# Attention scores in thirty-two-row products: sixteen 32 by 32 tiles of the TensorE array in place of four of 32 by 128

## The chip, the cores and the metric

The kernel runs on one core of a Trainium2 chip. The core has a matrix engine (TensorE, "PE" in the profile, with its weight loads shown as "PEld"), a vector engine (VectorE, DVE), a scalar engine (ScalarE, ACT), a general engine (GpSimd, POOL) and a sync engine (SyncE, SP) that here only issues DMA transfers. The metric is the device time of one execution in microseconds, as a median of several runs.

## What is computed

The reference is one block of a hybrid network on 16 sequences of 512 tokens by 256 features, all float32: causal attention with 16 heads of width 16, a routed feed-forward layer, a state-space scan, and the same routed layer once more, each on a layer-normalised input and added to the running `x`. The change touches attention alone:

```python
xn = x * rsqrt(mean(x * x) + EPS) * norm_w
q = (xn @ Wq.T + bq).reshape(B, T, H, hd).transpose(0, 2, 1, 3)
k = (xn @ Wk.T + bk).reshape(B, T, H, hd).transpose(0, 2, 1, 3)
v = (xn @ Wv.T + bv).reshape(B, T, H, hd).transpose(0, 2, 1, 3)
scores = einsum('bhqd,bhkd->bhqk', q, k) * scale
scores = where(causal, -inf, scores)
attn = softmax(scores, axis=-1)
out = einsum('bhqk,bhkd->bhqd', attn, v)
return xn + out.transpose(0, 2, 1, 3).reshape(B, T, D) @ Wo.T + bo
```

## The kernel before

**Order.** The program is written as a list of operations, each with an engine, a planned cost and the buffers that it reads and writes. `Plan.order` runs a small model of the engines over the list, and the operations are issued in the order that it picks, by due times written out in `STARTS` and `TURNS`. Each engine executes its own queue in that order. Attention of one sequence is thereby interleaved with the scan and the routed layers of the one or two before it. At the start, `Plan.resting` also adds some spare products (line 1056) that keep the array at work. Both use the planned costs, which are numbers in the source.

**Scores.** The 16 heads of a sequence are worked in four sets of four, and the sets in two pairs (the loop over `i`, line 723). For one set, queries and keys lie transposed in `qT` and `kT`: each of the four heads `g` has its own 32 partitions (`rows(g)`, line 517), so that a product over 32 partitions is one head's scores. Scores are computed twice. First with the queries' 128 rows as the stationary operand, for the row maxima (`maxima`, line 736, read by the VectorE reduction of line 749); then with the keys' 128 rows as the stationary operand and the maxima already subtracted in `qm`, for the exponentials (`weights`, line 685, read by the ScalarE exponential of line 689).

**The helper.** Both go through `filled` (line 635). It takes one buffer `sc` in PSUM, of 128 partitions by 4 heads by 512 columns, of which there is only one, and a list of one or two entries. An entry names a stationary block of 128 rows, a moving operand of `n` columns (512, 384, 256 or 128, because the causal triangle is skipped in blocks of 128), and a mask. For an entry, `score` (line 645) issues four products, one for each head; each writes all 128 partitions of that head's 512 columns. `masked` (line 652) then issues four bf16 products of 128 rows and 128 columns that add the causal mask on the diagonal block. Where the second entry has 128 columns, the mask is written first and the scores are added. The whole of a list is one operation of PE. It waits until the last reader of `sc` is done, and the reader (line 749 or 689) waits for the end of the operation.

For one pair of sets the lists are: four of one entry of 512 columns, four of 384 and 128 columns, and two of 256 and 256. That is 16 entries for one pair, 32 for a sequence and 512 in all, and each of the four widths occurs 128 times.

**Other products in small tiles.** The products of weights and values (line 672) and the sums of the scan (line 1020, and line 965 for its inputs) use 128 input partitions and 32 output rows: four tiles of the array side by side, each with its own 32 output partitions. Line 672 follows the exponentials; line 1020 follows GpSimd's product of line 1013.

Every float32 product above appears in the trace as two weight loads and two matmuls: line 647 has 2 x 2,048 of each for 512 entries of four products. Float32 transposes and the bf16 masks appear as one of each.

Of the kernel before, what the change touches and what calls it, by code (L numbers as in the profile page):

```python
# [17 lines left out]
P = 128  # L18
# [50 lines left out]
class Plan:  # L69
# [20 lines left out]
    def op(self, eng, cost, fn, r=(), w=(), lat=None, table=None, load=0.0, also=(), port=False, same=False):  # L90

        o = Op()
        self.slot += not same
        o.slot = self.slot
        o.eng, o.cost, o.fn, o.seq, o.num, o.table, o.load = eng, cost, fn, self.seq, len(self.ops), table, load
        o.lat = {"PE": 0.2, "SP": 2.0}.get(eng, 0.16) if lat is None else lat
        o.after, o.left, o.bufs = [], 0, []
        before = {}  # L100
        for things, writes in ((r, False), (w, True)):
            for thing in things:
                buf, part = thing if isinstance(thing, tuple) else (thing, None)
                if buf not in o.bufs:
                    o.bufs.append(buf)
                    buf.users += 1
                for p, (ws, rs) in buf.done.items():
                    if part is None or p is None or p == part:
                        for x in ws + (rs if writes else []):
                            before[x.num] = x  # L110
                ws, rs = buf.done.setdefault(part, ([], []))
                if not writes:
                    rs.append(o)
                elif part is None:
                    buf.done = {None: ([o], [])}
                else:
                    buf.done[part] = ([o], [])
        for buf in also:
            if buf not in o.bufs:
                o.bufs.append(buf)  # L120
                buf.users += 1
        before.pop(o.num, None)
        o.port, o.then, o.stage = port, None, self.stage
        for x in before.values():
            x.after.append(o)
            o.left += 1
        self.ops.append(o)
        return o
# [141 lines left out]
def tile_block(ctx: ExitStack, tc: tile.TileContext, a: dict, out: bass.AP):  # L270
# [4 lines left out]
    nc = tc.nc  # L275
# [6 lines left out]
    G = 4  # L282
# [218 lines left out]
    def psum(name):  # L501
        n, shape = banks[name]
        return plan.buf(name, lambda: ps.tile(shape, F32, tag=name, name=name, bufs=n))
# [13 lines left out]
    def rows(g):  # L517
        return slice(32 * g, 32 * g + 32)
# [10 lines left out]
    def pe(n, k=1, extra=0.02):  # L529

        return k * 2 * (n / 1200.0 + extra)
# [72 lines left out]
    def attention(b, x):  # L604
# [30 lines left out]
        def filled(todo, reads, into):  # L635


            sc = psum("sc")

            def run():  # L640
                for k, (lhsT, rhs, at, n, mask, diag) in enumerate(todo):

                    turned = k > 0 and n == P

                    def score():
                        for g in range(G):
                            nc.tensor.matmul(  # L647
                                sc()[:, g, at : at + n], lhsT=lhsT()[rows(g), :], rhs=rhs()[rows(g), :],
                                start=not turned, stop=turned,
                            )  # L650

                    def masked():
                        for g in range(G):
                            nc.tensor.matmul(  # L654
                                sc()[:, g, at + diag : at + diag + P], lhsT=identb, rhs=mask,
                                start=turned, stop=not turned,
                            )

                    for step in (masked, score) if turned else (score, masked):
                        step()  # L660

            return sc, op("PE", sum(pe(x[3], 1, 0.0) for x in todo) + (0.46 if len(todo) == 1 else 0.88 if todo[1][3] == P else 1.0), run, r=reads, w=[sc], also=into)
# [369 lines left out]
    for b in range(B):  # L1032
# [8 lines left out]
        n = NT // 2 if b == B - 1 else NT  # L1041
# [62 lines left out]
```

## Time and profile before

| what | value |
|---|---|
| time, median of 3 runs | 1951.58 us (1949.91 to 1952.15) |
| span of the profiled execution | 1952.9 us |
| mean granted TensorE clock | 0.968 |
| DVE busy | 1488.0 us (76%) |
| POOL busy | 1446.5 us (74%) |
| ACT busy | 1208.4 us (62%) |
| scores, line 647, matmul records | 4,096, of 210.3 + 211.8 us busy |
| masks, line 654, matmul records | 2,048, of 91.0 + 90.6 us busy |
| idle of PE just before line 647 | 54.2 + 45.3 us |
| DMA | 288.00 MB read, 26.21 MB written |
| instruction fetch of the largest queue (q8) | 105 packets, 1.72 MB |

The profile gives the span, from the first instruction to the last; of the profiled execution no separate time is shown. The span is 1.3 us above the median of the runs. "Busy" is the union of an engine's instructions, so that four products which run side by side count once. A row of a group gives the busy time of the whole group, the mean duration of one instruction in ns, and the idle time of its engine just before, with what ended it. Matmul durations include the time until the result has left the array.

### The profile page before, as it was taken

How to read it: one execution, taken by the hardware profiler on the slowest of the kernel's cores; microseconds unless marked ns; L12 is line 12 of the kernel's file. 1: busy time of each engine (PE TensorE's matmuls, PEld its weight loads, DVE VectorE, ACT ScalarE, POOL GpSimd, SP SyncE). 2: the span in 40 equal slices, each digit the busy share in tenths (PEclk: the TensorE clock that was granted, in tenths of full speed). 3: DMA queues.
4: the chain of work that ended last, by engine and by line, in shares of the span. 5: the costliest groups of instructions: out<-in, count | busy, mean ns of one | idle time of the engine just before them, and what ended most of it. 6: DMA issues, size and time to landing. Idle time of an engine off the chain costs nothing.

```text
span 1952.9 us, 34920 instructions
## 1 busy us (share of the span) xinstructions
PE 1710.2 (88%) x13337; PEld 953.1 (49%) x13337; DVE 1488.0 (76%) x2448; ACT 1208.4 (62%) x1618; POOL 1446.5 (74%) x846
## 2 busy tenths in 40 slices
PE   7889999999999989999899999999999999986445
PEld 5455445545454545545454555545454545544123
DVE  5245787879798887878798787879798787876553
ACT  2436466775757676675758576675758677573631
POOL 5102777878788887878788887878789787868893
PEclk9999899999999999999999999999999999998766
DMA  4002668768585768758585767768575877767891
GB/s 101 1 1 78 157 155 213 179 163 211 142 199 143 193 159 206 190 153 205 142 192 146 193 174 195 193 155 199 145 193 143 209 173 185 184 159 187 206 225 33
DMA packets 114568, 316.48 MB, mean 162 GB/s; under 512 B 17649, under 2 KB 38626, under 8 KB 114402
## 3 DMA queue, kind: packets, MB, share of 16 engines
q1 hardware_dynamic: 113554, 313.99, 65.1%
q8 instruction: 105, 1.72, 0.4%
q14 instruction: 61, 0.50, 0.1%
q10 hardware_dynamic: 848, 0.27, 0.1%
HBM read 288.00 MB, written 26.21 MB: 161 GB/s over the span
## 4 chain that ended last, share of the span: by engine, by line
PE 34%; DVE 25%; ACT 14%; issue 11%; POOL 10%; DMA 6%; SPq 0%; DVEq 0%; POOLq 0%; ACTq 0%
DVE dd L1010 10%; PE sc L647 7%; PE one L535 6%; PE one L579 6%; DVE negm L749 5%; DMA dd<-drows 5%; PE one L1020 5%; ACT one L1007 4%; PE one L672 4%; POOL dd L1013 4%; POOL dd L1002 3%; PE sc L654 2%; DVE st L542 2%; ACT xhR L555 2%; DVE x L594 2%
## 5 line engine op out<-in xcount | busy, mean ns | idle before, releaser
L1010 DVE TENSOR_TENSOR_SCAN dd<-one,dd 128x512 f32<-128x512 f32 x512 | 606.3, 1210 | 221.8 <-ACT one L1007 143.5
L1013 POOL TENSOR_TENSOR dd<-dd,bc 128x1024 f32<-128x1024 f32 x256 | 602.5, 2356 | 121.5 <-DVE dd L1010 55.4
L1002 POOL TENSOR_TENSOR dd<-dd,bc 128x1024 f32<-128x1024 f32 x256 | 604.1, 2361 | 86.3 <-DMA dd<-drows 63.0
L1007 ACT ACTIVATE one<-dd,am 128x512 f32<-128x512 f32 x512 | 345.7, 693 | 272.8 <-DVE dd L1010 136.0
L749 DVE TENSOR_REDUCE negm<-sc 128x4 f32<-128x1536 f32 (+3 forms) x224 | 368.1, 1667 | 68.4 <-PE sc L647 41.4
L647 PE MATMUL sc<-qm,kT 32*128 32x384 f32 (+3 forms) x2048 | 210.3, 480 | 54.2 <-ACT ptC L689 14.8
L647 PE MATMUL sc<-kT,qT 32*128 32x384 f32 (+3 forms) x2048 | 211.8, 482 | 45.3 <-DVE negm L749 43.6
L654 PEld LDWEIGHTS <-identb 128*128 128x128 bf16 x2048 | 115.4, 98 | 210.1 <-issue 210.1
L1020 PE MATMUL one<-dd,ysel 128*32 128x512 f32 x1024 | 153.1, 642 | 55.6 <-POOL dd L1013 49.3
L689 ACT ACTIVATE ptA<-sc 128x2048 f32<-128x2048 f32 x64 | 119.7, 1870 | 96.4 <-PE sc L654 96.4
L548 POOL TENSOR_SCALAR rs<-mv 128x4 f32<-128x4 f32 x64 | 12.4, 193 | 220.8 <-DVE mv L543 213.5
L647 PEld LDWEIGHTS sc<-qm,kT 32*128 32x128 f32 x2048 | 80.4, 183 | 134.7 <-ACT ptA L689 31.8
L647 PEld LDWEIGHTS sc<-kT,qT 32*128 32x128 f32 x2048 | 81.0, 183 | 128.2 <-DVE negm L749 56.4
L555 ACT ACTIVATE xhR<-x,nm,rs 128x256 f32<-128x256 f32 x192 | 102.3, 592 | 54.2 <-POOL nm L551 52.9
L689 ACT ACTIVATE ptB<-sc 128x2048 f32<-128x2048 f32 x64 | 120.0, 1875 | 23.7 <-PE sc L647 23.7
L535 PE MATMUL one<-base,xtR 128*128 128x256 f32 x496 | 133.9, 393 | 0.3 <-DVE dd L1010 0.2
L594 DVE TENSOR_TENSOR x<-one,x 128x512 f32<-128x512 f32 x126 | 83.8, 674 | 44.0 <-PE one L535 43.7
L542 DVE BATCH_NORM_STATS2 st<-x 128x6 f32<-128x256 f32 x256 | 103.2, 403 | 4.2 <-DMA x<-in_x_dram 2.5
L599 POOL TENSOR_TENSOR x<-x,bo 128x1024 f32<-128x1024 f32 x32 | 75.5, 2360 | 39.5 <-ACT xhA L555 30.5
L535 PEld LDWEIGHTS one<-base,xtR 128*128 128x128 f32 x496 | 92.2, 194 | 16.8 <-issue 1.7
L654 PE MATMUL sc<-mask_q,identb 128*128 128x128 bf16 x1024 | 91.0, 222 | 0.0
L654 PE MATMUL sc<-mask_k,identb 128*128 128x128 bf16 x1024 | 90.6, 221 | 0.0
(147 smaller groups left out, 2746.2 us busy)
## 6 DMA issues: line engine op xcount, KB each, us to landing
dd<-drows SPq DMA_DIRECT2D x512, 512.0 KB
x<-in_x_dram SPq DMA_DIRECT2D x16, 512.0 KB
drows<-dt SPq DMA_DIRECT2D x32, 256.0 KB
drows<-sg SPq DMA_DIRECT2D x32, 256.0 KB
bc<-brows SPq DMA_DIRECT2D x16, 512.0 KB
out_dram<-x SPq DMA_DIRECT2D x15, 512.0 KB
brows<-few SPq DMA_DIRECT2D x16, 64.0 KB
wo<-in_Wo_dram SPq DMA_DIRECT2D x2, 256.0 KB
```

Source lines behind the costliest of these rows:

```text
L535: nc.tensor.matmul(o[:, lo:hi], lhsT=lhsT, rhs=rhs, start=n == 0, stop=n == len(todo) - 1)
L542: nc.vector.bn_stats(st()[:, t, :], x()[:, t, :])
L555: op("ACT", act(256) + 0.23, lambda t=t: nc.scalar.activation(xh()[:, t, :], x()[:, t, :], AF.Identity, bias=nm()[:, t, 0:1], scale=rs()[: ...
L647: nc.tensor.matmul(sc()[:, g, at : at + n], lhsT=lhsT()[rows(g), :], rhs=rhs()[rows(g), :], start=not turned, stop=turned,)
L654: nc.tensor.matmul(sc()[:, g, at + diag : at + diag + P], lhsT=identb, rhs=mask, start=turned, stop=not turned,)
L689: o.then = op("ACT", act(G * 512), lambda: nc.scalar.activation(pt(), sc(), AF.Exp), r=[sc], w=[pt], table="exp")
L749: nc.vector.tensor_reduce(out, of, AX.X, ALU.max, negate=True)
L1002: op("POOL", pool(1024), lambda dd=dd: nc.gpsimd.tensor_tensor(dd()[:, :, 1, :], dd()[:, :, 1, :], both(0), ALU.mult), port=True, r=[(bc, ...
L1007: op("ACT", act(512) + 0.13, lambda i=i, k=k, dd=dd, dec=dec: nc.scalar.activation(dec(), dd()[:, i, 0, :], AF.Exp, scale=am[:, k + 4 * i ...
L1010: op("DVE", 1.13, lambda i=i, dd=dd, dec=dec: nc.vector.tensor_tensor_scan(dd()[:, i, 1, :], dec(), dd()[:, i, 1, :], 0.0, ALU.mult, ALU.a ...
L1013: op("POOL", pool(1024), lambda dd=dd: nc.gpsimd.tensor_tensor(dd()[:, :, 1, :], dd()[:, :, 1, :], both(1), ALU.mult), port=True, r=[(bc, ...
L1020: nc.tensor.matmul(sums()[rows(g), :], lhsT=ysel[:, m, :], rhs=four[g]()[:, g % 2, 1, :], start=m == 0, stop=m == 3)
```

## The change

In `score`, each head's product of 128 output rows becomes four products of 32 output rows. The stationary operand is cut to 32 columns, the output to 32 partitions; the moving operand is the same. The outer loop runs over the four blocks of output rows, the inner one over the four heads. The masks, the planned costs, the order of the operations and all waits between operations in the source are as before.

```diff
                     def score():
-                        for g in range(G):
-                            nc.tensor.matmul(
-                                sc()[:, g, at : at + n], lhsT=lhsT()[rows(g), :], rhs=rhs()[rows(g), :],
-                                start=not turned, stop=turned,
-                            )
+                        for h in range(0, P, 32):
+                            for g in range(G):
+                                nc.tensor.matmul(
+                                    sc()[h : h + 32, g, at : at + n], lhsT=lhsT()[rows(g), h : h + 32], rhs=rhs()[rows(g), :],
+                                    start=not turned, stop=turned,
+                                )
```

## The prediction

> **What bounds the kernel now.** I read the busy times first, then the chain of waits, then a table by stretches, then the score groups with their shapes kept apart.
>
> ```profile
> PE 1710.2 (88%) x13337; PEld 953.1 (49%) x13337; DVE 1488.0 (76%) x2448; ACT 1208.4 (62%) x1618; POOL 1446.5 (74%) x846
> ...
> PE 34%; DVE 25%; ACT 14%; issue 11%; POOL 10%; DMA 6%; SPq 0%; DVEq 0%; POOLq 0%; ACTq 0%
> ```
>
> PE is busiest, but the chain that ended last is shared among four engines. The 34% on PE are 664 us, or 0.39 of its 1710.2 us: if the chain stayed as it is, 0.39 of each microsecond added to PE would reach the end. A steady stretch, one sequence long (columns: length, then busy time and count of PE, PEld, DVE, ACT, POOL), says that the chain won't stay:
>
> ```profile
> 552.00:663.00 111.00, 102.32 (x832) 57.30 (x834) 92.62 (x152) 75.42 (x102) 91.36 (x53) 1.00 0.72 178
> ```
>
> PE is idle for only 8.7 of 111 us, so work added to it soon becomes the bound. The score products by width, and below them the tiles of 32 output rows that the kernel already has:
>
> ```profile
> L647 PE MATMUL sc<-kT,qT 32*128 32x512 f32 x512 | 74.0, 647 | 32.4 <-DVE negm L749 32.4
> L647 PE MATMUL sc<-kT,qT 32*128 32x384 f32 x512 | 59.4, 533 | 2.2 <-ACT ptB L689 1.6 <-DVE negm L749 0.4
> L647 PE MATMUL sc<-kT,qT 32*128 32x256 f32 x512 | 46.1, 426 | 10.7 <-DVE negm L749 10.7
> L647 PE MATMUL sc<-kT,qT 32*128 32x128 f32 x512 | 32.2, 321 | 0.0
> ...
> L672 PE MATMUL one<-ptA,vv 128*32 128x512 f32 x512 | 68.1, 603 | 9.0 <-DVE dd L1010 8.4
> L672 PE MATMUL one<-ptB,vv 128*32 128x384 f32 x512 | 54.2, 490 | 1.6 <-ACT ptB L689 1.6
> ```
>
> An entry (four products, two passes each) is 8 records, so 512 records are 64 entries: 74.0/64 = 1.156 us for 512 columns, 0.928 for 384, 0.720 for 256, 0.503 for 128. From 128 to 512 that is 0.653 us for 384 columns: 1.70 ns a column, 0.85 for each of two passes. The four heads therefore run side by side already. The tiles of 32 output rows do the same work in 68.1/64 = 1.064 and 54.2/64 = 0.847 us, some 0.08 less.
>
> **The change, part by part.** *Columns streamed.* Each of the sixteen tiles still streams n columns twice. If they overlap as the four do, the 1.70 ns a column stay: nothing is removed here, since the four heads filled all 128 rows of the array before.
>
> *Narrower weights.* A load brings 32 columns in place of 128. In the trace, the groups of eight loads look so:
>
> ```profile
> 603.35 0.31 PEld L647 LDWEIGHTS sc<-qm,kT 32*128 32x128 f32 x8 [0.17 <-issue]
> ...
> 601.33 0.16 PEld L1020 LDWEIGHTS one<-dd,ysel 128*32 128x32 f32 x8 [0.17 <-issue]
> ```
>
> The difference between the two rows of products, 0.08 us an entry, is what this saves. An isolated pair of groups agrees: 1.14 us for line 647 at 512 columns (599.48 us), 1.07 for line 1020 (601.33 us). I take -0.08.
>
> *Twelve more products, 24 more load and matmul pairs an entry.* In all 512 x 12 x 2 = 12,288 pairs, beside the 13,337 of now. The trace shows no entry with sixteen tiles, so this is bounded from both sides. The low end is the step from tile to tile in a burst that stands ready: eight loads of 110 ns take 0.16 us, so (160 - 110)/7 = 7 ns a step. Twelve more tiles start 12 x 7 = 84 ns later, and with -0.08 the entry stays as it is, about 0. The high end is the densest sustained row, the sixteen pairs of line 965: 398.02 to 398.49 us, where line 672 follows, or 29 ns a pair. That row is held by its 128 columns, so it is an upper bound of what the sequencer needs. At 29 ns with nothing queued ahead, the sixteenth product's first pass, pair 31 of 32, starts 30 x 29 = 870 ns late where the fourth tile's now starts 20 ns late: +0.85 - 0.08 = +0.77 us an entry.
>
> Between these stand the records of the sequencer's own waits. In more than a dozen sequences, four transposes of line 782 lie between two of them and pass in 74 ns: 18.5 ns a pair. In eight of twelve places where line 647 is followed by line 1020, sixteen pairs pass in 285 to 315 ns, about the same. At such waits at most 16 to 17 loads stood ahead of the array. I take these, because they measure the supply itself: of an entry's 32 pairs 17 stand ready while PE waits for `sc`, and the last first pass is (31 - 17) x 18.5 = 259 ns late. Per entry +0.259 - 0.020 - 0.08 = **+0.16 us**; for 512 entries +81 us of PE time.
>
> *What lies beside it.* An entry doesn't end before its last tile, and the masks can't start before. PE stands in its own order, so everything queued behind the entry waits too: masks, then whatever transpose, projection or scan sum the plan put there. The reader of `sc`, line 749 or 689, comes 0.16 us later for one entry and 0.32 for two; then the next score operation, which needs `sc` free. No DMA is moved and no queue of SP or POOL passed. Instruction fetch grows by 24,576 instructions; 1.72 MB for 26,674 is 64 bytes each, so 1.6 MB more, 0.4% of DMA time now and 0.8% after. I cost it at nothing, its cover being the seventeen loads that stand ready.
>
> *How much reaches the end.* Between 0.39 (the chain as it is) and 1 (PE bounds everything). I take 0.65: PE's 8.7 us of idle in 111 would take in some of the 81/16 = 5.1 us a sequence, but half of that idle, 56.3 us in all, is line 647 waiting for line 749, which the change puts off too. 81 x 0.65 = +53 us. The profile's span of 1952.9 lies 1.3 us above the median; 1951.6 + 53 = **2005 us**. Its own range, with 0.08 to 0.20 us an entry and 0.39 to 1: 1967 to 2054.
>
> *Two rules against the trace.* The trace first: at 257.87 us the third product of line 1020 waited for GpSimd, and the loads came in two fours, so both passes of the first two products stand in the queue before the third:
>
> ```profile
> 257.87 0.14 PEld L1020 LDWEIGHTS one<-dd,ysel 128*32 128x32 f32 x4 [0.33 <-issue]
> 258.85 0.14 PEld L1020 LDWEIGHTS one<-dd,ysel 128*32 128x32 f32 x4 [0.84 <-POOL dd L1013]
> ```
>
> Yet in line 647 four first passes start before any second one: within 603.30 to 603.50 us the trace has four matmuls in 0.60 us, each of 0.585. So a product passes over another tile's waiting second pass. The Trainium skill, "TensorE: Matmul & The Clock Gate", Part 3, says that matmuls start and end strictly in program order. By the trace the sum stands as above; by the rule each block of 32 rows would hold up the next, which is the second rival's price. The same page, Part 1, puts the least distance from start to start at about 25 ns; the 7 ns step above contradicts it for different tiles. By it, with nothing ready, an entry would gain 30 x 25 = 750 less 100 ns, 0.65 us, and the kernel 333 us of PE time. Its Part 3 also reports 10.6 times the speed for sixteen tiles of one pass at 4 ns a tile, which no run here shows.
>
> **The rivals.** *One: not slower.* If the supply keeps up with the burst, the step of 6 to 7 ns decides. 12 x 6 = 72 ns against 0.08 to 0.09 saved is -0.02 us an entry, -10 us of PE, -6 at the end: 1946; at 7 ns, no change. For it: one of the twelve places shows sixteen pairs in 131 ns, 8 ns a pair. It decides from about 8 ns a pair down: (31 - 17) x 8 = 112 ns less the 100 leave +0.012 us an entry, 6 us of PE, 4 at the end.
>
> *Two: the tiles of one head wait for each other.* If a second pass holds up the next block of rows in the same 32 partitions, the blocks form a chain of five passes in place of two. The columns of all entries are 128 x (512 + 384 + 256 + 128) = 163,840; three passes more at 0.85 ns are +418 us of PE, at 0.9 to 1 near the end: 2330 to 2370. For it: no trace of this kernel has more than three second passes waiting while a first one overtakes. Against it: tiles that share all input rows (line 1020) and tiles that share all output rows (line 647) both overlap. That the compiler lays the sixteen in fewer tiles would look the same, with other shapes in the rows.
>
> *Three: nothing stands ready.* If the queue is empty at each entry, because instructions are fetched too slowly or the doubled count eats the lead, the last first pass is 30 x 18.5 = 555 ns late: +0.455 us an entry, +233 us of PE, at 0.65 to 0.8: 2103 to 2138. Against it: PE waits for `sc` before many score operations, and the queue fills meanwhile.
>
> **How the numbers follow.** The forecast has 0.52; rival one 0.20, of which half is faster by over 0.2% and 0.08 within it; rival two 0.12; rival three 0.16. Some 0.2% (3.9 us) is what a measurement of this kernel can tell from no change. Faster 0.10, same 0.08, slower 0.82. The range reaches down to rival one's 1946 and up to just past rival three, 2145; it leaves out rival two and what lies below, under 0.2.
>
> **What would show it.** Right: line 647 with shapes 32*32 and 8,192 matmul records for each of its two pairs of operands; sixteen first passes of an entry of 512 columns begun within 0.2 to 0.3 us, and an entry 0.1 to 0.2 us longer than 1.156; PE's busy time up by some 80 us; idle before lines 749 and 689 for PE longer. Wrong towards rival one: sixteen starts within 0.11 us. Towards rival two: starts in fours, one pass apart, 2.1 us for 512 columns. Towards rival three: even steps of 18 ns or more for pairs through a whole entry, with "issue" before line 647. The share of 0.65 is wrong if PE's busy time rises as said and the span by much more or less.

## The result and the profile after

The changed kernel takes 1986.48 us (1985.95 to 1989.6), beside 1951.19 us before: 35 us more, a ratio of 1.0186 with a 95% interval of [1.0173, 1.0199]. The forecast was 2005 with a range of 1946 to 2145. Direction and range held; the reason did not. (The two profiled spans differ by less, 31.3 us: in the other runs a span lies about 2 us below its execution's time, so the profiled execution of the kernel before, with a span of 1952.9 us, was some 3.5 us longer than the median.)

The page of the changed kernel: span, busy time of the engines, the queue that brings PE's instructions (packets, MB, share of DMA time) and the chain of waits.

```profile
span 1984.2 us, 59496 instructions
...
PE 1727.9 (87%) x25625; PEld 919.9 (46%) x25625; DVE 1489.6 (75%) x2448; ACT 1210.7 (61%) x1618; POOL 1450.3 (73%) x846
...
q8 instruction: 201, 3.29, 0.8%
...
PE 37%; DVE 22%; ACT 16%; issue 13%; POOL 10%; DMA 3%; SPq 0%; DVEq 0%; POOLq 0%; ACTq 0%
```

The 96 additional packets of q8, of 16,384 bytes or 256 x 64 each, are just the 24,576 additional instructions.

PE's busy time rose by 17.7 us, not by 81, and its idle time by 13.6: together the 31.3 us by which the span grew. The scores by width, now at line 648 (64 entries a row), below one row of before:

```profile
L647 PE MATMUL sc<-qm,kT 32*128 32x128 f32 x512 | 32.2, 321 | 0.0
...
L648 PE MATMUL sc<-kT,qT 32*32 32x512 f32 x2048 | 74.3, 599 | 31.5 <-DVE negm L750 31.5
...
L648 PE MATMUL sc<-kT,qT 32*32 32x384 f32 x2048 | 60.2, 493 | 2.4 <-ACT ptB L690 1.9 <-DVE negm L750 0.5
...
L648 PE MATMUL sc<-kT,qT 32*32 32x256 f32 x2048 | 46.2, 386 | 10.9 <-DVE negm L750 10.9
...
L648 PE MATMUL sc<-qm,kT 32*32 32x128 f32 x2048 | 35.5, 282 | 16.5 <-issue 16.5
...
L648 PE MATMUL sc<-kT,qT 32*32 32x128 f32 x2048 | 32.1, 280 | 0.0
```

The rows of `kT,qT` stood at 74.0, 59.4, 46.1 and 32.2 us before. An entry of sixteen tiles takes as long as one of four. The row of `qm,kT` at 128 columns does not: 35.5 where it was 32.2 us, and 16.5 us of idle time before it that no instruction's end explains ("issue"), where there was none.

One undisturbed entry, first a stretch of 0.12 us at its start and then its weight loads:

```profile
611.15 0.60 PE L648 MATMUL sc<-qm,kT 32*32 32x384 f32 x16
...
611.15 0.23 PEld L648 LDWEIGHTS sc<-qm,kT 32*32 32x32 f32 x32 [0.17 <-issue]
```

All sixteen first passes, of 505 ns each, lie within 0.60 us: (600 - 505)/15 = 6 to 7 ns from start to start. The 32 loads take 0.23 us. And one disturbed entry (start, length, group):

```profile
432.64 0.62 PE L655 MATMUL sc<-mask_k,identb 128*128 128x128 bf16 x8
433.19 0.49 PE L648 MATMUL sc<-qm,kT 32*32 32x128 f32 x29
436.11 0.41 PE L648 MATMUL sc<-qm,kT 32*32 32x128 f32 x3 [2.43 <-issue]
436.45 0.66 PE L709 MATMUL one<-ident,avs 128*128 128x128 f32 x4
```

PE stops after 29 of 32 matmuls of one entry and goes on 2.4 us after the last of them has ended, 2.7 us after its start. The stretches around it (length, then busy time and count of PE, PEld, DVE, ACT, POOL; last the clock, the DMA share and GB/s):

```profile
425.00:433.30 8.30, 6.58 (x159) 3.76 (x143) 6.95 (x18) 8.29 (x11) 6.05 (x4) 1.00 1.04 243
433.30:434.60 1.30, 0.38 (x29) 0.12 (x28) 0.88 (x1) 0.09 (x1) 1.30 (x2) 1.00 0.73 173
434.60:436.10 1.50, 0.00 (x0) 0.00 (x0) 0.00 (x0) 0.00 (x0) 1.50 (x1) 1.00 0.07 22
```

For 8 us the scan's transfers hold all 16 DMA engines (share 1.04). At 433.30 us a packet of PE's instructions starts, the first since 424.9 us. Then PE, VectorE and ScalarE all stand still; GpSimd works on. The other long stops look alike: at 197.0, 659.0, 885.0 and 1101.7 us a packet starts, from 1.0 us before the last matmul ahead of the stop to 0.2 us behind it, and PE goes on 2.7 to 2.8 us after that start, though a packet itself takes 1.26 us.

How much of the 31.3 us is this? I took for every score entry the time from its first to its last matmul start, and what it has over the shortest entry of its width. Worked out from single records:

```
columns   before: shortest, sum over it    after: shortest, sum over it
128         232 ns    0.2 us                 233 ns   19.6 us
256         339 ns    0.6 us                 340 ns    0.6 us
384         445 ns    0.2 us                 446 ns    5.7 us
512         552 ns    0.7 us                 553 ns    5.5 us
```

The undisturbed entries are equal to 1 ns. The disturbed ones have lost 31.4 us, beside 1.7 before: 29.7 us of the 31.3 by which the span grew. 28.6 of the 31.4 lie in the entries for the exponentials. Not all of it is idle time, since matmuls that began before a stop run on; 17.3 us are (total, times, longest):

```profile
PE sc L648 <- issue: 17.3, 10, 2.7
```

Single records also tell where PE stops. Number all records of PE (weight loads, matmuls and its own waits) in the order of their starts. The eight gaps of over 1 us inside entries come after record 5,569, 12,225, 18,625, 25,025, 31,169, 37,569, 43,969 and 50,369. Each of these is 193 more than a multiple of 256, the number of instructions in a packet. So the stops lie whole packets apart, at the places where one packet ends and the next begins.

### The profile page after: what moved, and what is told of

Its sections match the earlier page's. It is cut to its first block, busy times and chain, and to the rows that moved or that the text cites. A ratio compares the mean times of both kernels' runs of the same rounds, so it can differ in the third digit from the quotient of the medians.

```text
span 1984.2 us, 59496 instructions
## 1 busy us (share of the span) xinstructions
PE 1727.9 (87%) x25625; PEld 919.9 (46%) x25625; DVE 1489.6 (75%) x2448; ACT 1210.7 (61%) x1618; POOL 1450.3 (73%) x846
## 4 chain that ended last, share of the span: by engine, by line
PE 37%; DVE 22%; ACT 16%; issue 13%; POOL 10%; DMA 3%; SPq 0%; DVEq 0%; POOLq 0%; ACTq 0%
PE sc L648 9%; DVE dd L1011 8%; PE one L535 6%; PE one L579 6%; DVE negm L750 5%; PE one L1021 5%; POOL dd L1014 4%; ACT one L1008 4%; PE one L673 4%; PE sc L655 3%; POOL dd L1003 3%; DMA dd<-drows 3%; DVE st L542 2%; ACT ptB L690 2%; DVE x L594 2%
## 5 line engine op out<-in xcount | busy, mean ns | idle before, releaser
L648 PE MATMUL sc<-qm,kT 32*32 32x512 f32 (+3 forms) x8192 | 222.6, 444 | 72.5 <-issue 17.3
L648 PE MATMUL sc<-kT,qT 32*32 32x256 f32 (+3 forms) x8192 | 212.8, 439 | 44.8 <-DVE negm L750 42.9
L648 PEld LDWEIGHTS sc<-qm,kT 32*32 32x32 f32 x8192 | 64.3, 103 | 153.7 <-issue 36.8
L648 PEld LDWEIGHTS sc<-kT,qT 32*32 32x32 f32 x8192 | 61.9, 103 | 128.1 <-DVE negm L750 53.3
```

Of the source, the lines that this page charges most:

```text
L648: nc.tensor.matmul(sc()[h : h + 32, g, at : at + n], lhsT=lhsT()[rows(g), h : h + 32], rhs=rhs()[rows(g), :], start=not turned, stop=turned,)
```

## The experiments

Theory A: PE's instructions come too late. The change nearly doubles their bytes, packets are held up while the scan's transfers fill the DMA engines, and PE runs dry in the dense score products. The rivals: every pair has a price of its own (B), entries pay by their width, the narrow ones most (C), blocks of one head hold each other up (D), sixteen narrow tiles cost time as such (E), instruction fetch is too slow even without other traffic (F), the number of instructions alone sets the loss (G).

**A third of the pairs.** The step of the loop over rows, and the size of the slices, is 64:

```diff
-                        for h in range(0, P, 32):
+                        for h in range(0, P, 64):
```

> Score products of 64 output rows: eight in place of four, 4,096 load and matmul pairs more than before (a third of what the change adds). Theory A (instruction packets that come late behind the data transfers stop PE for 2 to 3 us at a time): packets rise from 105 to about 137, so PE runs dry seldom; stalls inside score groups sum to 0 to 5 us and the time is 1945 to 1957 us. Theory B (every additional pair has its price in the entry where it stands): a third of +35, so 1960 to 1966 us.

Measured: 1945.29 us beside 1950.74, ratio 0.9974 [0.9965, 0.9984]: faster than the changed kernel, and by 0.3% than the one before. 137 packets, stalls inside score groups 1.6 us. Its maxima entries:

```profile
L648 PE MATMUL sc<-kT,qT 32*64 32x512 f32 x1024 | 72.3, 619 | 32.4 <-DVE negm L750 32.4
...
L648 PE MATMUL sc<-kT,qT 32*64 32x384 f32 x1024 | 57.7, 507 | 2.2 <-ACT ptB L690 1.8 <-DVE negm L750 0.5
L648 PE MATMUL sc<-kT,qT 32*64 32x256 f32 x1024 | 44.9, 407 | 10.8 <-DVE negm L750 10.8
...
L648 PE MATMUL sc<-kT,qT 32*64 32x128 f32 x1024 | 30.4, 293 | 0.0
```

72.3/64 = 1.130 us where it was 1.156, and so for each width: 0.02 to 0.03 us an entry. A narrower load is gained and only four more tiles are to be started. PE's busy time falls by 13.4 us (1710.2 to 1696.8), the time by 5.5: 0.41 reaches the end. B, which wanted +9 to +15, falls.

**One width alone.** The narrow tiles where `n == 512`, and where `n == 128`, in two kernels:

```diff
+                        size = 32 if n == 512 else P
-                        for h in range(0, P, 32):
+                        for h in range(0, P, size):
```

> Thirty-two-row products in the 128 entries of 512 columns alone: 3,072 pairs more than before. Theory A: packets about 129, hardly a stall, time within 4 us of before (1947 to 1956). Theory B: a quarter of +35, 1957 to 1963. Theory C (entries pay by width, because second passes of narrow ones come before the supply): under 2 us, since 512 columns give the supply the longest time.

> Thirty-two-row products in the 128 entries of 128 columns alone: 3,072 pairs more than before, as many as with 512 columns alone. Theory A: as with 512 alone, within 5 us of before, because the number of instructions is the same. Theory B: +9 us. Theory C: the 19.6 us that the groups of 128 columns lose in the changed kernel stay, 1965 to 1975.

Measured: 1949.86 (ratio 0.9994 [0.9982, 1.0007]) and 1951.99 us (1.0007 [0.9995, 1.0019]), neither to be told from before. In the second, all 128 entries of 128 columns take 233 or 234 ns from first to last start, where the changed kernel loses 19.6 us: C falls.

**The loops exchanged.**

```diff
-                        for h in range(0, P, 32):
-                            for g in range(G):
+                        for g in range(G):
+                            for h in range(0, P, 32):
```

> The changed kernel with the two loops exchanged: the four row blocks of one head follow each other, then the next head. Theory A: instruction bytes are the same, so 1980 to 1992 us, and sixteen starts 7 ns apart. Theory D (blocks that share input rows hold each other up, and only the order of the change spares them): the groups get longer by one pass or more and the time rises over 2050 us.

Measured: 1996.02 us (1985.55 to 1997.18, ratio 1.0225 [1.0194, 1.0256]). The median lies above what A named, though the fastest run equals the changed kernel's. The shortest entries are the same to the ns (233, 340, 446, 553) and the disturbed ones lose 30.4 us in the profiled execution, whose span is 1983.5. D falls; what made most of its other executions 10 us longer stays open.

**As many instructions in other tiles.** Sixteen products an entry, of 64 rows and half of the columns:

```diff
+                        order = (0, n // 2) if diag else (n // 2, 0)
+                        for c in order:
+                            for h in range(0, P, 64):
...
+                                        sc()[h : h + 64, g, at + c : at + c + n // 2], lhsT=lhsT()[rows(g), h : h + 64],
+                                        rhs=rhs()[rows(g), c : c + n // 2], start=not turned, stop=c == order[turned],
```

> Sixteen products an entry as in the changed kernel, but of another shape: 64 output rows and half of the columns each, in eight tiles. Theory A (late instruction packets): as many instructions and 201 packets, so the stalls are there again, 1970 to 1995 us. Theory E (the price lies in the sixteen narrow tiles): no stalls, the time of the kernel with 64 output rows, 1940 to 1952 us.

Measured: 1985.53 us, ratio 1.0170 [1.0155, 1.0186], 30.9 us of stalls. Without a single 32 by 32 tile, the loss is that of the change. E falls: it is the instructions, not the shape of the tiles.

**Either half of the entries.** The narrow tiles for the exponentials alone (`mask is mask_k`), and for the maxima alone (`mask is mask_q`), 6,144 pairs more each:

```diff
+                        size = 32 if mask is mask_k else P
-                        for h in range(0, P, 32):
+                        for h in range(0, P, size):
```

> Thirty-two-row products only where the scores for the exponentials are computed, in 256 of 512 entries: 6,144 pairs more than before, half of the change. Theory A: about 153 packets; the lateness of a packet has to outlast two packets of instructions, so the cost is far under one half, 0 to 10 us (1949 to 1960). Theory B (a price for every pair): +17 us, 1966 to 1970.

> Thirty-two-row products only where the scores for the row maxima are computed: 6,144 pairs more than before, as many as in the kernel that had them for the exponentials alone (1982 us). Theory A in its sharper form (a late packet costs only where score products for the exponentials run during a burst of the scan's transfers): the eight stalls of 2 to 3 us are gone and the time is 1948 to 1960 us. Theory G (the number of additional instructions sets the loss, wherever they stand): 1976 to 1986 us, as in the other half.

Measured: 1982.31 us (ratio 1.0155 [1.0138, 1.0172]) for the exponentials, 1951.47 (1.0001 [0.9988, 1.0013]) for the maxima. The first is a miss: I had expected 0 to +10 and it is +30. With 153 packets in both, one half pays nearly the whole loss and the other nothing. So neither B nor G holds, and theory A as I first had it, in which fewer bytes would do, was too simple. What decides is where the instructions stand; in the changed kernel too the loss lay in the exponentials' entries. The exponentials' kernel stops at the same place of the program as the changed one, after the same 29 matmuls:

```profile
431.80 0.62 PE L656 MATMUL sc<-mask_k,identb 128*128 128x128 bf16 x8
432.36 0.49 PE L649 MATMUL sc<-qm,kT 32*32 32x128 f32 x29
435.33 0.41 PE L649 MATMUL sc<-qm,kT 32*32 32x128 f32 x3 [2.48 <-issue]
```

**Half of the scan's traffic**, in the kernel before and in the changed one:

```diff
-                            out=dd()[:, i].rearrange("p d t -> p (d t)"),
-                            in_=lines.unsqueeze(0).to_broadcast([NS, 8, 2 * T]),
+                            out=dd()[:, i, 0, :],
+                            in_=lines.unsqueeze(0).to_broadcast([NS, 8, T]),
...
-                        dd()[:, :, 1, :], dd()[:, :, 1, :], both(0), ALU.mult
+                        dd()[:, :, 1, :], dd()[:, :, 0, :], both(0), ALU.mult
```

> The kernel before with half of the scan's data traffic: only the rows of dt are fetched, not those of their products with xc, and GpSimd multiplies dt in their place (the scan's input lacks the factor xc). Same instructions otherwise. It is the base for the next kernel; all theories: 1930 to 1952 us.

> The changed kernel with half of the scan's data traffic, the same way (the scan's input lacks the factor xc). Theory A (packets are late because they wait behind the scan's transfers): with bursts half as long, the distance to the kernel before with half traffic falls from 35 us to under 10, and hardly a PE stall over 1 us is left. Theory F (the fetch is too slow for dense instructions by itself, whatever the data traffic): the distance stays at 30 to 40 us.

Measured: 1944.31 and 1952.56 us. The distance between four and sixteen tiles falls from 35 to 8 us, with the same 201 packets. F falls, and the scan's transfers are shown to be a cause. Around the place of the stop above, the changed kernel with half traffic reads:

```profile
424.00:433.00 9.00, 6.79 (x148) 3.88 (x148) 5.71 (x11) 8.99 (x13) 5.17 (x3) 1.00 0.01 2
```

A DMA share of 0.01 where it was 1.04. One long stop is left, at 197.9 us; all entries together lose 6.5 us.

**The packets shifted against the program.** 64 and 32 tiny transposes ahead of everything:

```diff
+        for _ in range(64):
+            nc.tensor.transpose(one[0:8, 256:264], ident[0:8, 0:8], ident[0:8, 0:8])
```

> The changed kernel with 64 tiny transposes of 8 by 8 ahead of everything, while PE waits for weights: 128 instructions, half a packet of 256, so that every later packet ends half a packet earlier in the program. Theory A: where a packet ends within the dense stretch decides who stalls, so the eight long stalls at 29 of 32 matmuls move or go, and the time changes by more than 5 us either way (1955 to 2000, not 1986 +- 4). Theory G: 1983 to 1990 as before the shift.

> The same with 32 tiny transposes, 64 instructions, a quarter of a packet. Theory A: again another sum of stalls than the changed kernel's and than with half a packet, the stall of 2 to 3 us now 64 instructions earlier or later in the program or gone; 1955 to 2000 us. Theory G: 1983 to 1990.

Measured: 1989.78 us (ratio 1.0212 [1.0187, 1.0237]) and 1985.55 (1.0185 [1.0165, 1.0204]). The time did not move by more than 5 us, so this part of A's expectation missed. Its "eight long stalls at 29 of 32 matmuls" were also misread: the eight come after 31, 29, 22, 15, 28, 21, 14 and 31 matmuls, and only the one at 433 us after 29. The stops did move. The place at 433 us is undisturbed with half a packet:

```profile
437.20 0.50 PE L650 MATMUL sc<-qm,kT 32*32 32x128 f32 x32
437.63 0.66 PE L711 MATMUL one<-ident,avs 128*128 128x128 f32 x4
```

The long stops are now at 548.5, 774.4, 990.5, 1215.7, 1439.6 and 1664.9 us, in the sequences that had no long one. Counted in the same way, the gaps of over 1 us inside score entries lie again 193 records beyond a multiple of 256, here and in every other kernel that has such gaps: 47 of 47 in seven kernels, each ending 2.5 to 3.0 us after the start of a packet. So PE waits at the end of one packet for a later one, and which entry pays depends on where packets end. The sum hardly does: gaps of over 0.3 us at packet ends that end 2.3 to 3.2 us after a packet's start, in whatever operation of PE, make 29.3 us in the changed kernel, 30.8 and 31.5 in the two shifted ones and none before.

All kernels side by side. "Most between" is the largest number of PE instructions begun between the starts of two packets; a packet of 16,384 bytes holds 256 of 64 bytes. The last column sums what score entries take over the shortest of their kind, in one profiled execution each; stops in other operations, of which the shifted kernels have more, are not in it:

```
kernel                                packets   most between   time us   stalls us
before                                    105            356   1951.19         1.7
changed                                   201            526   1986.48        31.4
64 rows                                   137            412   1945.29         1.6
32 rows, 512 columns alone                129            377   1949.86         1.7
32 rows, 128 columns alone                130            392   1951.99         0.6
loops exchanged                           201            518   1996.02        30.4
64 rows, half columns                     201            522   1985.53        30.9
32 rows, exponentials alone               153            536   1982.31        26.4
32 rows, maxima alone                     153            418   1951.47         2.4
shift of 128 instructions                 202            501   1989.78        26.0
shift of 64 instructions                  202            498   1985.55        24.3
before, half traffic                      105            308   1944.31         1.3
changed, half traffic                     201            437   1952.56         6.5
```

The times are medians; each was compared with runs of the kernel before beside it (1950.74 to 1952.39). In every kernel that loses some 30 us or more, the largest number is 498 to 536, about two packets of instructions; every other one stays at 437 or below. In the changed kernel, the 89 packets that had a DMA share of 1.0 or more in the 3 us before them came on average after 310 instructions, at most after 526; the 64 that had under 0.3, after 211 and at most 387.

## Why the prediction came out as it did

*What bounds the kernel* held as far as it was tested: work taken off PE reached the end at 0.41 with 64 rows, where the chain's share gave 0.39. The share of 0.65 for added work stays untested, since the change added none to speak of. A stop of PE's supply passes nearly whole, as VectorE and ScalarE stood still with PE at 434.60 us: 29.7 us more of stalls, 31.3 us more of span.

*Columns streamed* and *narrower weights* held: the streaming is the same, and the weights pay for the tiles. Only the sum of the two is measured, 233 ns beside 232 from first to last start.

*Twelve more products* is a step that failed. "17 stand ready" and 18.5 ns a pair made +0.16 us an entry and +81 us of PE. In the trace, the sixteen tiles of an undisturbed entry start 6 to 7 ns apart, so the low end of that bound, about 0, was the true value. All sixteen first passes began within 0.10 us, which the prediction had named as the sign of rival one (0.11), where its own was 0.2 to 0.3. The records of the sequencer's waits gave a rate for an instruction that follows a separate wait; I took it for the rate at which a whole entry is supplied, and no row showed that.

*What lies beside it* is the step that failed most. Of instruction fetch it says "I cost it at nothing, its cover being the seventeen loads that stand ready". By its own upper bound of 29 ns a pair that cover is 0.5 us long at most, and PE stood idle for up to 2.7 us at a packet's end. Nearly the whole loss is in the term that I set to 0. The sizes were both wrong and partly made up for each other: 81 x 0.65 forecast, about 31 x 1 measured. That the direction came out right is therefore luck: by the price of an entry alone, the time would have stayed at that of before, as it did with narrow tiles at 512 columns, at 128 columns or for the maxima alone (1949.86, 1951.99 and 1951.47 us).

*The rivals.* Rival one had the price of an entry right and missed what follows from the instructions. Rival two fell with the equal lengths of undisturbed entries. Rival three named the cause, instructions fetched too slowly, but priced it on every entry: 233 us of PE. It showed itself in 13 entries that are longer by over 0.5 us, eight of them at one place of the program, and its own sign ("issue" before the score line) is in the trace with 16.5 us.

*Two rules against the trace.* The Trainium skill's page "TensorE: Matmul & The Clock Gate", Part 3, has matmuls start in program order. The sixteen first passes at 611.15 us, with each product's second pass between them in the program, contradict it for different tiles. The same Part's 4 ns a tile for packed tiles is nearer to the 6 to 7 ns here than the 25 ns from start to start in Part 1.

What stays open: how far ahead instruction packets are asked for, and in which queue they wait. The runs show that less other traffic removes most of the stops, that PE stops at the end of a packet, and that about two packets' worth of instructions pass before it does; that two packets stand ready is only inferred from this.

## What to carry to other kernels

Cutting a product into more tiles is paid for in instructions as well as in array time: count the bytes of the engine's program, and look where the densest stretch of it meets the longest burst of transfers. "Issue" before a group that waits for nobody, with the engines that need it idle and a DMA share of 1 just before, is what a late instruction packet looked like here. A gain from narrower weights can still be had with half the cut: 64 rows gave the saving without the stalls.

## What the runs showed of the hardware

- Sixteen 32 by 32 tiles with two float32 passes each overlap as fully as four wide ones: 233 ns from first to last start at 128 columns, 232 ns for four tiles of 32 by 128, in either order of the loops.
- After a gap of over 1 us inside a score entry, PE goes on 2.5 to 3.0 us after the start of a packet of instructions, about twice the packet's own 1.26 us. All 47 such gaps lie where a packet of 256 instructions ends.
- Shifting the program by 64 or 128 instructions moves the stops to other sequences and leaves the time within 4 us of 1986.
